# Copying the attention context out of PSUM in two VectorE operations, with the zero column set by GpSimd

## The chip, the cores and the metric

The kernel runs on one core of a Trainium2 chip. The metric is the device time of one execution in microseconds (us). The engines that matter here are TensorE (PE; its weight loads are shown apart as PEld), VectorE (DVE), ScalarE (ACT), GpSimd (POOL) and the DMA queue of SyncE (SP). Each engine works through its own queue of instructions in order and waits at an instruction until the semaphores it names have been raised by the others.

## The reference

A block of cross attention with a feed-forward part, for 128 sequences of 128 tokens with 256 channels, 16 heads of 16 channels, all in float32. The mask is strict (`mask` is 0 below): a token attends only to earlier tokens, so the first token of a sequence attends to none, and its attention row is set to zero.

```python
q = (query @ Wq + bq).reshape(b, s, N_HEADS, D_K).transpose(0, 2, 1, 3)
...
scores = jnp.einsum('bhqd,bhkd->bhqk', q, k) / jnp.sqrt(jnp.float32(D_K))
allowed = j < i + mask
scores = jnp.where(allowed, scores, NEG_INF)
attn = jax.nn.softmax(scores, axis=-1)
attn = attn.at[:, :, 0, :].set(0.0)
ctx = jnp.einsum('bhqk,bhkd->bhqd', attn, v)
...
attn_out = ctx @ Wo + bo
x = layer_norm(query + attn_out, ln1_g, ln1_b)
ffn = jax.nn.relu(x @ W1 + b1) @ W2 + b2
out = layer_norm(x + ffn, ln2_g, ln2_b)
```

The context of the first token is therefore zero in every sequence and every head.

## The kernel before

The 128 sequences are taken in 64 pairs p. The steps of several pairs are interleaved: step p works on the scores of pair p, the context and output projection of pair p - 2, the first feed-forward product of pair p - 3 and p - 4, the second of p - 4 and p - 5, and the projections of pair p + 1. Steps 9 to 60 come from a loop, `for p in range(9, 61): step(p)`; what comes before and after is written out by hand.

The order of the work is fixed by hand. The schedule is manual, and `step` goes through a list of keys, `ORDER`, and calls for each key a small function that issues its instructions. Each engine's queue holds its instructions in just the order in which they are issued, whatever they wait for. The stretch of the list around the change reads (a suffix -1 means the pair of one step earlier):

```python
weigh addbo re0-2 vr-1 hf-2 re2-2 re1-2 turnx-1 xc2-1 re3-2 context scores res0 ro3-2
ro0-2 br1 maskA0 ro2-2 add3 oc0 ro1-2 v1 maskA1 oc2 maskB hs0-1 o1 max3 vk1 vk0 q1
lowmax eh7 oc1 v2 br0 xs2-1 qk w1-1 hs1-1 ok eh6 tokc-1 w2-1 tokx vk2 el3 oc3 hs3-1 v3
add1 el4 w5-1 max1 br3 el0 add2 o2 cc0 wk-1 eh3 k1 finish1-1 ...
```

What these keys do, as far as the prediction speaks of them:

- `weigh` multiplies the exponentials with the values on TensorE (L586, L596) into a PSUM bank. The columns of that bank are ordered by half of the channels, sequence, and token, where the token's index is split as l, q, a (2 x 2 x 32).
- `context` (function at L607) multiplies that bank with `inv`, the inverse sums of the softmax, into the tile `cxT` in SBUF, on VectorE. `cxT` is one tile (128 partitions x 512 columns) for the whole kernel; it is set to zero once at the start (L146 to L148). The column of the first token (l = q = a = 0) of each of the four column groups is never written after that, and so stays zero. For that the function writes the half with q = 1 in one operation of 256 columns (L612) and the half with q = 0 in two (L617): 4 x 31 columns without the first token, and 4 x 32.
- `res0` and `res1` (L1608) make on GpSimd the residual of the second half, `x1b`, from the normed tokens `x1` of pair p - 3, in two operations of 512 columns.
- The matrix products use Strassen's scheme in its form with seven products, so sums and differences of blocks of the operands are formed on GpSimd: `oc0` to `oc3` of `cxT` (L1534), `cc0` to `cc3` of the turned context tokens `cT` (L1534), `xc` of `xT`, `hs` of the hidden layer (`hS`, L1547), `xs` of `x1` (`xS`, L1636). TensorE reads them in `o1` to `o4` (output projection; `o1` takes `cxT` and `oc0`), `k1` to `k4` (keys; `k1` takes `cc0`), `q1` to `q4`, `w1` to `w7` and `h1` to `h7`, most of them at L1147 and L1358.
- `scores` are the products of queries and keys (L440); `maskA0`, `maskA1` and `maskB` add the mask on VectorE (L464, L456).

Of the kernel before, what the change touches and what calls it, by code (L numbers as in the profile page):

```python
# [10 lines left out]
ALU = mybir.AluOpType  # L11
# [8 lines left out]
def tile_cross_attention_block(  # L20
# [22 lines left out]
    nc = tc.nc  # L43
# [101 lines left out]
    cxT = const.tile([P, KC, 2, P], F32, tag="cxT", name="cxT")  # L145
# [460 lines left out]
    def context(p):  # L606
        if "inv" in states[p]:  # L607
            parts = "p (m s l q a) -> p m s l q a"
            pc = states[p].pop("pc").rearrange(parts, m=KC, s=2, l=2, q=2)
            to = cxT.rearrange("p m s (l q a) -> p m s l q a", l=2, q=2)  # L610
            inv = states[p].pop("inv")
            nc.vector.tensor_tensor(  # L612
                to[:, :, :, :, 1], pc[:, :, :, :, 1], inv[:, :, :, :, 1], ALU.mult
            )
            for l in range(2):
                at = slice(1 - l, 32)
                nc.vector.tensor_tensor(  # L617
                    to[:, :, :, l, 0, at], pc[:, :, :, l, 0, at], inv[:, :, :, l, 0, at], ALU.mult
                )
            return  # L620
        pc = states[p].pop("pc").rearrange("p (u i) -> p u i", i=P)
        nc.scalar.copy(cxT.rearrange("p m s i -> p (m s) i")[:, :, 1:], pc[:, :, 1:])
# [1015 lines left out]
    def bring_part(p, n):  # L1638
# [4 lines left out]
        "weigh": lambda p: weigh(p - 2),  # L1643
        "scores": lambda p: scores_both(p),
        "context": lambda p: context(p - 2),
        "deviations": lambda p: scales_of(p),
        "means": lambda p: means_of(p),
# [249 lines left out]
    exponential(1, 1, ONE)  # L1897
    weigh(0)
    context(0)
    project_queries(2)  # L1900
    maximum(1, 1, TWO)
# [62 lines left out]
    weigh(1)  # L1964
    bring(2, nc.sync, EVERY[:8])
    context(1)
    residual1(0)
    scores(3, 1)
# [1124 lines left out]
```

## Time and profile before

| | |
|---|---|
| time, median of 3 runs | 1478.79 us (1475.64 to 1478.85) |
| span of the profiled execution, first to last instruction | 1476.0 us |
| TensorE matmul / weight load busy | 1450.0 us (98%) / 1394.3 us (94%) |
| VectorE busy | 1372.8 us (93%) |
| ScalarE busy | 1304.3 us (88%) |
| GpSimd busy | 1266.4 us (86%) |
| context on VectorE, 256 columns (L612) | 59 operations, median 424 ns |
| context on VectorE, 124 and 128 columns (L617) | 118 operations, median 277 ns |

The page gives the profiled execution by its span; it has no other time of its own. It lies 2.8 us below the median of the runs and inside their range.

Rows of the timeline read: start in us from the span's start, duration in us, engine, line, operation, tile written <- tiles read, type of the operands, number of operations that were merged into the row, and in brackets the idle time of the engine just before the row with what ended it. Rows of a view of groups have the count and the minimum, median and maximum in ns. Rows by stretch have: the stretch, its length, and the busy time (with the number of instructions) of PE, PEld, DVE, ACT and POOL, then TensorE's granted clock, the busy share of the DMA engines and GB/s. A row of waits reads: who waited <- for whom, total us, times, longest.

### The profile page before, as it was taken

The page shows a single profiled execution, that of the slowest core. Times are in us where ns is not written, and L with a number is a line of the kernel's source. Part 1 is how long each engine was busy: PE and PEld are TensorE (multiplying, and loading weights), DVE is VectorE, ACT ScalarE, POOL GpSimd, SP SyncE. Part 2 cuts the span into 40 slices and gives each one's busy share as a digit, 9 for nine tenths or more (in the row PEclk, how much of TensorE's full clock was granted, in tenths as well). Part 3 has the DMA queues.
Part 4 walks back from the last instruction along what each step waited for, and adds up shares of the span by engine and source line. Part 5 has one row for each costly group of instructions (what it writes and reads, how often), then busy time and mean ns, then how long its engine had stood idle before and what let it go on. Part 6 is the DMA issues. An engine that isn't in the chain of part 4 may idle for free.

```text
span 1476.0 us, 61938 instructions
## 1 busy us (share of the span) xinstructions
PE 1450.0 (98%) x20713; PEld 1394.3 (94%) x20713; DVE 1372.8 (93%) x3231; ACT 1304.3 (88%) x5559; POOL 1266.4 (86%) x1816
## 2 busy tenths in 40 slices
PE   8999899999999999999999999999999999999998
PEld 7778799999999999999999999999999999999988
DVE  6987999999999999999999999999999999999767
ACT  4659899999999999999999999999999999999743
POOL 5986898988988988988988988888898888887966
PEclk9999999999999999999999999999999999999999
DMA  8274766766766767776766766766776766774541
GB/s 202 66 142 104 178 162 149 159 152 156 167 158 155 154 152 157 169 159 152 165 147 151 166 157 157 163 149 153 163 160 157 161 147 154 163 163 113 130 109 51
DMA packets 367448, 220.33 MB, mean 149 GB/s; under 512 B 279600, under 2 KB 335152, under 8 KB 367152
## 3 DMA queue, kind: packets, MB, share of 16 engines
q1 hardware_dynamic: 364864, 214.27, 63.9%
q8 instruction: 187, 3.06, 0.9%
q10 hardware_dynamic: 2288, 2.11, 0.7%
q14 instruction: 109, 0.89, 0.2%
HBM read 55.06 MB, written 18.09 MB: 50 GB/s over the span
## 4 chain that ended last, share of the span: by engine, by line
PE 72%; ACT 7%; DVE 4%; DMA 3%; SPq 1%; POOL 1%; issue 1%; DVEq 0%; ACTq 0%; POOLq 0%
PE banks L1147 40%; PE banks L1358 20%; PE banks L440 5%; ACT sm L931 5%; PE banks L596 3%; DMA kT<-kr 2%; PE banks L586 2%; PE banks L971 1%; DMA brought<-turned 1%; ACT kr L1213 1%; PE banks L869 0%; PE banks L1044 0%; ACT qT L1175 0%; SPq L552 0%; PE banks L629 0%
## 5 line engine op out<-in xcount | busy, mean ns | idle before, releaser
L931 ACT ACTIVATE sm<-banks,nmx 128x128 f32<-128x128 f32 x944 | 336.8, 383 | 15.8 <-DVE nmx L1558 12.6
L931 ACT ACTIVATE sm<-sm,nmx 128x64 f32<-128x64 f32 x944 | 321.6, 369 | 1.4 <-DVE nmx L920 1.4
L533 DVE STREAM_TRANSPOSE turned<-sm 128x1024 f32<-128x1024 f32 x186 | 217.0, 1213 | 3.3 <-DMA brought<-turned 2.4
L931 ACT ACTIVATION_READ_ACCUMULATOR sm<-banks,nmx 128x1 f32 x944 | 211.4, 224 | 0.0
L931 ACT ACTIVATION_READ_ACCUMULATOR sm<-sm,nmx 128x1 f32 x944 | 207.8, 220 | 0.0
L1147 PE MATMUL banks<-wt,hS 128*128 128x128 f32 x1344 | 177.6, 275 | 0.0
L1358 PE MATMUL banks<-xS,w1t 128*128 128x128 f32 x1344 | 177.2, 275 | 0.0
L1147 PEld LDWEIGHTS banks<-wt,hS 128*128 128x128 f32 x1344 | 163.6, 192 | 0.1
L1358 PEld LDWEIGHTS banks<-xS,w1t 128*128 128x128 f32 x1344 | 163.4, 192 | 0.0
L1558 DVE TENSOR_REDUCE nmx<-banks 128x4 f32<-128x512 f32 x224 | 152.1, 679 | 1.9
L1547 POOL TENSOR_TENSOR hS<-hT 128x512 f32<-128x512 f32 x116 | 147.5, 1273 | 5.4 <-ACT hT L876 2.4
L1358 PE MATMUL banks<-brought,w 128*128 128x128 f32 x896 | 118.2, 275 | 0.0
L1608 POOL TENSOR_TENSOR x1b<-x,g_r 128x512 f32<-128x512 f32 x56 | 72.3, 1291 | 51.0 <-ACT x L703 51.0
L1147 PE MATMUL banks<-w,hT 128*128 128x128 f32 x896 | 109.8, 275 | 0.0
L1358 PEld LDWEIGHTS banks<-brought,w 128*128 128x128 f32 x896 | 109.0, 192 | 0.0
L440 PE MATMUL banks<-kT,qT 32*64 32x128 f32 (+1 forms) x3840 | 100.7, 331 | 6.3 <-DMA kT<-kr 3.7
L1147 PEld LDWEIGHTS banks<-w,hT 128*128 128x128 f32 x896 | 104.8, 192 | 0.1
L440 PEld LDWEIGHTS banks<-kT,qT 32*64 32x64 f32 x3840 | 82.7, 131 | 16.9 <-ACT hT L1399 4.9
L1534 POOL TENSOR_TENSOR oc<-cxT 128x128 f32<-128x128 f32 x112 | 49.0, 457 | 57.9 <-DVE cxT L617 56.9
L1387 ACT ACTIVATE hT<-hT,b1e_c 128x256 f32<-128x256 f32 x224 | 95.7, 509 | 1.2 <-DVE hT L1383 1.1
L1552 DVE TENSOR_TENSOR banks<-banks,neg 128x256 f32<-128x256 f32 x224 | 93.1, 416 | 0.0
L703 ACT ACTIVATE x<-t,nb,sd 128x256 f32<-128x256 f32 x126 | 68.4, 592 | 19.1 <-POOL nb L726 11.9
(322 smaller groups left out, 4841.1 us busy)
## 6 DMA issues: line engine op xcount, KB each, us to landing
brought<-turned SPq DMA_DIRECT2D x936, 128.0 KB, 2.4
out_dram<-t SPq DMA_DIRECT2D x63, 256.0 KB, 4.7
xb<-in_x_dram SPq DMA_DIRECT2D x124, 128.0 KB, 3.2
cb<-in_ctx_dram SPq DMA_DIRECT2D x124, 128.0 KB, 3.2
x<-in_x_dram SPq DMA_DIRECT2D x31, 512.0 KB, 5.4
kT<-kr SPq DMA_DIRECT2D x112, 128.0 KB, 2.7
brought<-turned SPq DMA_DIRECT2D x40, 96.0 KB, 2.2
w<-in_L_xattn_W_dram SPq DMA_DIRECT2D x2, 1024.0 KB, 7.8
```

The source lines that it names most:

```text
L440: nc.tensor.matmul(st["sps", hi][r][s * HP : (s + 1) * HP, m * 2 * n : (m + 1) * 2 * n].rearrange("p (e j) -> p e j", e=2), st["qT"][strip ...
L533: nc.vector.transpose(turned[:, :, at : at + 256].rearrange("p j (n a) -> p n j a", a=32), states[p]["sm", hi].rearrange("p h j -> p (h j) ...
L703: nc.scalar.activation(x1[:, s], t1[:, s], AF.Identity, bias=st["nb", 1][:, s], scale=sd[:, s])
L931: nc.scalar.activation(sm[:, h, :], src, AF.Exp, bias=nmx[:, h : h + 1], scale=1.0, **({"accum_out": st["su"][:, at : at + 1]} if summed e ...
L1147: nc.tensor.matmul(out, left(k) if self.depth > 1 else left, right(k) if self.depth > 1 else right, start=(n == 1 and k == 0), stop=(k == ...
L1358: nc.tensor.matmul(ps[:, i * P : (i + 1) * P].rearrange("p (n a) -> p n a", a=32), left(i), right, start=(n in (1, 2, 5) and i == 0), stop ...
L1387: nc.scalar.activation(self.hT[:, f, at], self.hT[:, f, at] if src is None else src, AF.Relu, bias=b1e_c[:, f : f + 1], scale=1.0,)
L1534: nc.gpsimd.tensor_tensor(c[:, n], left, right, how)
L1547: engine.tensor_tensor(c[:, n], left, right, how)
L1552: nc.vector.tensor_tensor(ps[:, :, HP:], ps[:, :, HP:], neg[:, 1, None, :].to_broadcast([P, 4, HP]), ALU.add)
L1558: nc.vector.tensor_reduce(states[p]["nmx", 1][:, 4 * b : 4 * b + 4], banks[:, b].rearrange("p (n j) -> p n j", j=P), AX.X, ALU.max, negate ...
L1608: nc.gpsimd.tensor_tensor(st["x1b"], st["x1b"] if n else st["x1"], (be1b_r if n else g1_r)[:, None, :].to_broadcast([P, 2, D]), ALU.add if ...
```

## The change

The two operations on the half with q = 0 become one over all of its 256 columns, so VectorE now writes the first token's columns as well. GpSimd then sets these four columns (one per column group) to zero again, each time, in an instruction that is issued directly behind VectorE's two, within the same function.

```diff
             pc = states[p].pop("pc").rearrange(parts, m=KC, s=2, l=2, q=2)
             to = cxT.rearrange("p m s (l q a) -> p m s l q a", l=2, q=2)
             inv = states[p].pop("inv")
-            nc.vector.tensor_tensor(
-                to[:, :, :, :, 1], pc[:, :, :, :, 1], inv[:, :, :, :, 1], ALU.mult
-            )
-            for l in range(2):
-                at = slice(1 - l, 32)
+            for q in range(2):
                 nc.vector.tensor_tensor(
-                    to[:, :, :, l, 0, at], pc[:, :, :, l, 0, at], inv[:, :, :, l, 0, at], ALU.mult
+                    to[:, :, :, :, q], pc[:, :, :, :, q], inv[:, :, :, :, q], ALU.mult
                 )
+            nc.gpsimd.memset(cxT[:, :, :, 0:1], 0.0)
             return
```

On GpSimd, around the context of one step of the loop, the queue held before (the names are the tiles written <- read, their numbers count buffers; in brackets the semaphores waited for):

```order
L295 TENSOR_TENSOR x_12322<-x_12322,bov_r 128x512 [waits DMAHW0_49]
L1534 TENSOR_TENSOR xc_12756<-xT_12609 128x128
L1608 TENSOR_TENSOR x1b_12979<-x_28_12876,g_r 128x512 [waits DVE_49,Activation_49]
L1534 TENSOR_TENSOR oc_12990<-cxT 128x128 [waits DVE_49]
L1534 TENSOR_TENSOR oc_12990<-cxT 128x128
L1547 TENSOR_TENSOR hS_13002<-hT 128x512 [waits PE_49,Activation_49]
L1534 TENSOR_TENSOR oc_12990<-oc_12990,cxT 128x128 [waits Pool_49]
```

and it now holds (lines behind the change are 3 lower):

```order
L295 TENSOR_TENSOR x_12322<-x_12322,bov_r 128x512 [waits DMAHW0_49]
L1531 TENSOR_TENSOR xc_12756<-xT_12609 128x128
L616 MEMSET cxT 128x4 [waits DVE_49]
L1605 TENSOR_TENSOR x1b_12979<-x_28_12876,g_r 128x512 [waits Activation_49]
L1531 TENSOR_TENSOR oc_12990<-cxT 128x128 [waits DVE_49,Pool_49]
L1531 TENSOR_TENSOR oc_12990<-cxT 128x128
L1544 TENSOR_TENSOR hS_13002<-hT 128x512 [waits PE_49,Activation_49]
L1531 TENSOR_TENSOR oc_12990<-oc_12990,cxT 128x128 [waits Pool_49]
```

The memset stands ahead of `x1b`, because `context` comes before `res0` in the list of keys; the wait for VectorE, which stood at the first `oc`, now stands one operation of 512 columns earlier.

On TensorE, where the output projection begins, the queue held before:

```order
L1147 MATMUL banks<-wv,cT_9419 128x128
L1147 MATMUL banks<-wvt,cc_9463 128x128
L253 NO_OP x3
L1147 MATMUL banks<-wo,cxT 128x128 [waits DVE_49]
L1147 MATMUL banks<-wo,cxT 128x128
L1147 MATMUL banks<-wot,oc_9813 128x128 [waits Pool_49]
```

and it now holds:

```order
L1144 MATMUL banks<-wv,cT_9419 128x128
L1144 MATMUL banks<-wvt,cc_9463 128x128
L253 NO_OP x3
L1144 MATMUL banks<-wo,cxT 128x128 [waits DVE_49,Pool_49]
L1144 MATMUL banks<-wo,cxT 128x128
L1144 MATMUL banks<-wot,oc_9813 128x128 [waits Pool_49]
```

Nothing moved there; the first product on `cxT` has a second semaphore to wait for, that of GpSimd.

## The prediction

> **What bounds the kernel now.** I read the page's engine shares first, then the chain of waits, then the same shares in two stretches (540 us of the loop, and one step).
>
> ```profile
> PE 1450.0 (98%) x20713; PEld 1394.3 (94%) x20713; DVE 1372.8 (93%) x3231; ACT 1304.3 (88%) x5559; POOL 1266.4 (86%) x1816
> PE 72%; ACT 7%; DVE 4%; DMA 3%; SPq 1%; POOL 1%; issue 1%; DVEq 0%; ACTq 0%; POOLq 0%
> ...
> 800.00:1340.00 540.00, 538.00 (x8088) 527.05 (x8087) 520.75 (x1267) 509.49 (x2232) 475.21 (x706) 1.00 0.69 156
> 804.94:826.96 22.02, 22.02 (x337) 21.58 (x334) 21.29 (x53) 20.88 (x93) 19.57 (x29) 1.00 0.73 169
> ```
>
> PE is busy for all 22.02 us of a step at a granted clock of 1.00; GpSimd (POOL) has the most room, 22.02 - 19.57 = 2.45 us. That room makes the change look free, so I looked at where it lies. The view of who waited for whom, for POOL:
>
> ```profile
> POOL oc L1534 <- DVE cxT L617: 56.9, 54, 1.5
> POOL x1b L1608 <- ACT x L703: 51.0, 51, 1.4
> ```
>
> About 1.05 us per step goes before `oc`, which waits for the context, and 1.0 us before `x1b`, the first residual product, which stands ahead of `oc`. The rest of POOL's step has no room. The timeline of POOL, VectorE (DVE) and TensorE (PEld is its weight load) around one context:
>
> ```profile
> 803.11 0.46 POOL L1534 TENSOR_TENSOR xc<-xT 128x128 f32<-128x128 f32 x1
> 804.94 1.29 POOL L1608 TENSOR_TENSOR x1b<-x,g_r 128x512 f32<-128x512 f32 x1 [1.37 <-ACT x L703]
> 806.41 0.42 DVE L612 TENSOR_TENSOR cxT<-banks,brought 128x256 f32<-128x256 f32 x1
> 806.75 0.47 DVE L617 TENSOR_TENSOR cxT<-banks,brought 128x124 f32<-128x124 f32 x2
> 807.14 0.42 DVE L464 TENSOR_TENSOR sm<-banks,neg 128x256 f32<-128x256 f32 x1
> 807.30 0.87 POOL L1534 TENSOR_TENSOR oc<-cxT 128x128 f32<-128x128 f32 x2 [1.07 <-DVE cxT L617]
> 808.19 1.27 POOL L1547 TENSOR_TENSOR hS<-hT 128x512 f32<-128x512 f32 x1
> 808.53 0.53 PEld L1147 LDWEIGHTS banks<-wo,cxT 128*128 128x128 f32 x4
> 808.98 0.30 PEld L1147 LDWEIGHTS banks<-wot,oc 128*128 128x128 f32 x2
> 809.42 0.46 POOL L1534 TENSOR_TENSOR oc<-oc,cxT 128x128 f32<-128x128 f32 x1
> 809.83 0.46 POOL L1636 TENSOR_TENSOR xS<-brought 128x128 f32<-128x128 f32 x1
> 810.25 1.28 POOL L1547 TENSOR_TENSOR hS<-hS,hT 128x512 f32<-128x512 f32 x1
> 811.48 0.47 POOL L1534 TENSOR_TENSOR oc<-cxT,oc 128x128 f32<-128x128 f32 x1
> 811.89 1.28 POOL L1547 TENSOR_TENSOR hS<-hT,hS 128x512 f32<-128x512 f32 x1
> 813.12 0.47 POOL L1534 TENSOR_TENSOR cc<-cT 128x128 f32<-128x128 f32 x1
> 814.11 0.30 PEld L1147 LDWEIGHTS banks<-cc,wkt 128*128 128x128 f32 x2
> ```
>
> From `oc` at 807.30 to `cc` at 813.12 POOL runs without a gap. TensorE takes the first `oc` 808.98 - (807.30 + 0.46) = 1.22 us after it is done (0.46 is the length of the like operations), and the first `cc` 814.11 - 813.59 = 0.52 us after. That 0.52 us is the narrowest place on which this forecast rests.
>
> **The change, term by term.** In VectorE's queue the two operations of 124 and 128 columns become one of 256. Starts are 0.34 us apart behind the 256-column operation (806.41 to 806.75) and the whole context holds VectorE for 0.73 us (to 807.14); two operations of 256 hold it for 2 x 0.34 = 0.68 us. The context ends at 806.75 + 0.42 = 807.17 instead of 806.75 + 0.47 = 807.22: 0.05 us sooner. VectorE works beside a full TensorE, so this gain alone is worth no more than 0.05 us a step. [...]
>
> In POOL's queue the order of instructions shows the memset ahead of `x1b`, and it must wait for VectorE's second operation. So everything that is queued behind it now waits for the context too: first `x1b` (1.29 us), which used to run while POOL had nothing else to do, and behind that `oc`, `hS`, `xS` and `cc`. The memset itself is not in this loop; the nearest rows are POOL's at the start of the program:
>
> ```profile
> 0.72 0.10 POOL L144 MEMSET power<- 128x4 f32 x1 [0.29 <-POOLq L3074]
> 0.75 0.20 POOL masks.py:197 MEMSET ident<- 128x128 f32 x1
> ```
>
> The same four columns, contiguous, take 0.10 us and the next starts after 0.03; 128 columns take 0.20. The bounds are 0.03 and 0.20 us, and I take 0.10, the duration of the row with the same count. Below nothing is excluded, since it is work added to one queue.
>
> `oc` started 807.30 - 807.22 = 0.08 us after the context. The memset then starts at 807.17 + 0.08 = 807.25, `x1b` at 807.35, and `oc` one operation of 512 columns later, 1.24 us by the starts of the two that follow each other here:
>
> ```profile
> 800.63 1.28 POOL L1608 TENSOR_TENSOR x1b<-x1b,be1b_r 128x512 f32<-128x512 f32 x1
> 801.87 1.28 POOL L295 TENSOR_TENSOR x<-x,bov_r 128x512 f32<-128x512 f32 x1
> ```
>
> That is 808.59, or 1.29 us late (bounds 1.22 and 1.39 with the memset's). POOL has no gap before `cc`, so `cc` ends at 813.59 + 1.29 = 814.88. How long after that TensorE starts is bounded by two places where it stood waiting for POOL:
>
> ```profile
> 1451.28 0.46 POOL L1636 TENSOR_TENSOR xS<-xS,cb 128x128 f32<-128x128 f32 x1
> 1451.79 0.30 PEld L1044 LDWEIGHTS banks<-xS,w1t 128*128 128x128 f32 x2 [0.71 <-POOL xS L1636]
> ...
> 43.89 1.90 POOL L500 TENSOR_TENSOR turned<-turned,rs 128x1024 f32<-128x1024 f32 x1
> 46.01 0.31 PEld L569 LDWEIGHTS banks<-ident,turned 128*128 128x128 f32 x3 [0.64 <-POOL turned L500]
> ```
>
> 0.05 us behind the operation of this size, 0.22 us behind a larger one; I take 0.10, nearer the first. TensorE would load `cc` at 814.98 instead of 814.11 and stand still for 0.87 us, a part of it (808.59 + 0.46 + 0.10 - 808.98 = 0.17 us) already at `oc`. The matmuls on `cxT` itself have to wait for the memset, done by 807.35, well before 808.53. The pause is the delay plus the start behind POOL less the 0.52 us that were spare; with the bounds of both it lies between 1.22 + 0.05 - 0.52 = 0.75 and 1.39 + 0.22 - 0.52 = 1.09 us.
>
> Is the pause paid back within the step? A pause that is already there answers it:
>
> ```profile
> 783.85 0.42 DVE L612 TENSOR_TENSOR cxT<-banks,brought 128x256 f32<-128x256 f32 x1
> 784.31 1.05 PE L440 MATMUL banks<-kT,qT 32*64 32x128 f32 x33 [0.53 <-DMA kT<-kr]
> ```
>
> From 783.85 to the next context at 806.41 are 22.56 us, 0.53 more than 22.03: it was not paid back. The next value that is late after `cc` is its last part, due 1.07 us after it is made:
>
> ```profile
> 816.83 0.46 POOL L1534 TENSOR_TENSOR cc<-cT,cc 128x128 f32<-128x128 f32 x1
> 818.36 0.30 PEld L1147 LDWEIGHTS banks<-cc,wk 128*128 128x128 f32 x2
> ```
>
> After the first pause TensorE comes 0.87 us later and POOL 1.29, which leaves 1.07 + 0.87 - 1.29 = 0.65 us: no second pause.
>
> The loop runs p from 9 to 60, 52 steps with this order: 52 x 0.87 = 45.2 us. Pauses that lie between a context and `cc` run beside POOL's work and are swallowed by the new one:
>
> ```profile
> PE banks L440 <- DMA kT<-kr: 3.7, 6, 0.9
> PE banks L440 <- ACT hT L1399: 0.5, 2, 0.3
> ```
>
> So 45.2 - 4.2 = 41 us remain. Outside the loop I add nothing. The last memset waits for the context that ends near 1430.3 and holds back two operations on `t`; behind them POOL stood idle anyway:
>
> ```profile
> 1426.13 1.27 POOL L758 TENSOR_TENSOR t<-t,g_r 128x512 f32<-128x512 f32 x1 [1.86 <-ACT t L740]
> ...
> 1435.24 0.23 POOL L651 TENSOR_SCALAR ve<-mv 128x2 f32<-128x2 f32 x1 [6.49 <-DVE mv L645]
> ```
>
> The profiled execution's span is 1476.0 us and would become 1517. The runs shown have their median 2.8 us above that span, so the forecast is 1478.8 + 41 = 1520 us, slower by 2.8%. With the pause's bounds it is 1478.8 + 52 x 0.75 - 4.2 = 1514 to 1478.8 + 52 x 1.09 - 4.2 = 1531.
>
> **The rivals.**
>
> *It is not slower.* If VectorE, busy for 21.29 of 22.02 us, sets the step, the 0.05 us saved there counts, 52 x 0.05 = 2.6 us, and the time is 1476. It decides if POOL's delay stays below 0.52 us, which would need `x1b` to take some 0.4 us instead of 1.29. For it speaks POOL's 2.45 us of room in each step; against it, that the room lies before the memset, not between it and `cc`.
>
> *Only `oc` is felt.* If POOL made up its delay between `oc` and `cc`, the pause would be the 0.17 us at `oc`, 52 x 0.17 = 9 us, 1488. Against it: the unbroken rows from 807.30 to 813.12.
>
> *The memset is dear.* If it held POOL 0.5 us, the pause grows by 0.4 and the time to 1520 + 52 x 0.4 = 1541. Neither of the two rows above is near that, though neither writes four columns that lie 128 apart.
>
> *The pauses cost TensorE its clock.* In the stretch with its long wait near the end the granted clock was down; where it paused for shorter times it was not:
>
> ```profile
> 150.00:158.00 8.00, 5.96 (x42) 5.10 (x42) 6.52 (x18) 8.00 (x46) 6.07 (x10) 1.00 0.82 185
> 1425.00:1428.00 3.00, 1.12 (x44) 1.13 (x48) 0.00 (x0) 1.52 (x4) 1.79 (x2) 0.68 0.65 161
> ```
>
> At 0.68 over 3 us a pause would cost 0.96 us more, 52 x 0.96 = 50 us, 1570. The first row, 2.04 us of idle in 8 at 1.00, speaks against it. [...]
>
> That the memset stands elsewhere than the source has it is excluded by the order of instructions.
>
> **Chances.** Forecast 0.76; not slower 0.08 (0.03 of it faster, 0.05 the same); `oc` alone 0.06; dear memset 0.07; clock 0.03. A difference counts from 0.3%, 4.4 us, about what a measurement of this kernel can tell. So faster 0.03, same 0.05, slower 0.92. The likeliest case's own 1514 to 1531 is widened toward its neighbours, to 1505 and 1538, for the unknown start after POOL and the unseen memset.
>
> **What would show it.** Right: in the changed loop POOL's `x1b` starts behind the memset with POOL idle for about 3 us before the memset; `oc` starts 1.3 us later against the context; TensorE waits for POOL's `cc` in nearly every step, some 0.9 us, and contexts lie 22.9 us apart. VectorE's busy time falls by about 59 x 0.05 = 3 us. Wrong: a step still near 22.0 us, or a wait that TensorE shows elsewhere than at `cc`.

## The result, and the profile after

| | before | after |
|---|---|---|
| time, median | 1478.4 us (1475.6 to 1478.9) | 1501.0 us (1500.7 to 1501.8) |
| span of the profiled execution | 1476.0 us | 1498.8 us |
| the 52 steps of the loop, from the trace | 1150.1 us | 1172.6 us |
| usual step, up to 860 us | 22.03 us | 22.37 to 22.39 us |

The changed kernel is slower: after to before 1.016, with a 95% interval of 1.0146 to 1.0175, or 22.6 us. The forecast was 1520 us with a range from 1505 to 1538. The sign and the place were right; the time lies 4 us below the range. A step is counted here from the end of the context on VectorE to the end of the next. Of the 22.8 us between the two spans 22.5 lie in the 52 steps of the loop.

The engine shares and the chain of waits of the changed kernel's page, which answer to the first two lines of the prediction:

```profile
PE 1458.8 (97%) x20713; PEld 1396.0 (93%) x20713; DVE 1372.7 (92%) x3172; ACT 1310.1 (87%) x5559; POOL 1266.4 (84%) x1875
PE 55%; POOL 14%; DVE 6%; ACT 5%; DMA 4%; issue 3%; SPq 1%; POOLq 0%; DVEq 0%; ACTq 0%
```

POOL had 1% of the chain and has 14%, though its busy time is the same to the tenth: it is on the path because of when it works, not how much. "issue", time in which an engine waits for nothing that the profile shows, went from 1% to 3%. That is the first trace of something that the prediction didn't have. The longest of POOL's waits:

```profile
POOL cxT L616 <- DVE cxT L613: 140.8, 57, 5.6
```

Both waits of POOL, for `x1` and for the context, have become one at the memset, 2.5 us on average and 2.8 us in the step shown below. The waits of TensorE's weight loads between 270 and 860 us, and between 970 and 1340 us:

```profile
PEld banks L1144 <- POOL cc L1531: 6.1, 19, 0.4
PEld banks L440 <- ACT hT L1396: 4.6, 6, 1.0
PEld banks L1144 <- DVE sm L464: 4.5, 26, 0.2
```

```profile
PEld banks L440 <- ACT hT L1396: 4.6, 5, 1.2
PEld banks L1144 <- DVE sm L464: 4.2, 15, 1.2
PEld banks L1144 <- issue: 3.6, 7, 0.7
PEld banks L440 <- issue: 1.8, 2, 0.9
```

In the first stretch TensorE waits for POOL's `cc`, as forecast, but for about 0.33 us a time and not 0.87. In the second stretch no wait for `cc` is listed; TensorE stands at other places, up to 1.2 us, for "issue" or for a `sm` that had long been done. The rows for `hT` are the same pauses before the scores that the matmuls' view puts down to the keys (`kT`); the kernel before has them too (1.6 us in 2 times and 1.7 in 3 in the same stretches), and what makes them come and go stays open below. Most steps are 22.37 to 22.39 us in the first stretch; in the second they reach 23.1 us.

The timeline of one step of the first stretch, for VectorE, POOL and the weight loads around `cc`:

```profile
814.85 0.76 DVE L613 TENSOR_TENSOR cxT<-banks,brought 128x256 f32<-128x256 f32 x2
815.59 0.42 DVE L464 TENSOR_TENSOR sm<-banks,neg 128x256 f32<-128x256 f32 x1
...
815.33 0.10 POOL L616 MEMSET cxT<- 128x4 f32 x1 [2.82 <-DVE cxT L613]
815.40 1.28 POOL L1605 TENSOR_TENSOR x1b<-x,g_r 128x512 f32<-128x512 f32 x1
816.63 0.87 POOL L1531 TENSOR_TENSOR oc<-cxT 128x128 f32<-128x128 f32 x2
817.46 1.27 POOL L1544 TENSOR_TENSOR hS<-hT 128x512 f32<-128x512 f32 x1
...
822.39 0.47 POOL L1531 TENSOR_TENSOR cc<-cT 128x128 f32<-128x128 f32 x1
...
822.05 0.53 PEld L1144 LDWEIGHTS banks<-cT,wk 128*128 128x128 f32 x4
822.91 0.30 PEld L1144 LDWEIGHTS banks<-cc,wkt 128*128 128x128 f32 x2 [0.34 <-POOL cc L1531]
```

The context's two operations run from 814.85 to 815.61; one of them takes 0.42 us, so the first is done at 815.27. The memset starts at 815.33, 0.06 us behind the first and before the second is done. It doesn't wait for the second. POOL takes `x1b` behind it, as the queue has them: `x1b` starts 0.07 us behind the memset's start, where before it ran 1.47 us ahead of the context (804.94 against 806.41).

### The profile page after: what moved, and what is told of

Its sections match the earlier page's. It is cut to its first block, busy times and chain, and to the rows that moved or that the text cites. A ratio compares the mean times of both kernels' runs of the same rounds, so it can differ in the third digit from the quotient of the medians.

```text
span 1498.8 us, 61994 instructions
## 1 busy us (share of the span) xinstructions
PE 1458.8 (97%) x20713; PEld 1396.0 (93%) x20713; DVE 1372.7 (92%) x3172; ACT 1310.1 (87%) x5559; POOL 1266.4 (84%) x1875
## 4 chain that ended last, share of the span: by engine, by line
PE 55%; POOL 14%; DVE 6%; ACT 5%; DMA 4%; issue 3%; SPq 1%; POOLq 0%; DVEq 0%; ACTq 0%
PE banks L1144 30%; PE banks L1355 17%; POOL hS L1544 6%; DMA kT<-kr 4%; ACT sm L928 3%; PE banks L440 3%; POOL oc L1531 1%; POOL xS L1633 1%; POOL cc L1531 1%; PE banks L968 1%; PE banks L596 1%; DVE turned L1611 1%; DVE hT L1380 1%; DVE hT L1394 1%; DVE cxT L613 1%
## 5 line engine op out<-in xcount | busy, mean ns | idle before, releaser
L616 POOL MEMSET cxT<- 128x4 f32 x59 | 6.2, 105 | 140.8 <-DVE cxT L613 140.8
L1290 DVE TENSOR_TENSOR t<-banks,x1b 128x256 f32<-128x256 f32 x168 | 53.1, 316 | 48.8 <-PE banks L1144 38.6
```

Source lines behind the costliest of these rows:

```text
L1290: nc.vector.tensor_tensor(to, src, of, ALU.add)
```

## The experiments

`EMPTY` is the table with the number of NO_OPs that TensorE's queue gets behind each named product. Where an expectation says that a NO_OP stands in front of `v1` or `h4`, it is the one issued behind that product; behind `v1` stand 3 in the kernels before and after the change. All runs, each with the kernel before on the same chip (medians 1475.5 us for rows 1, 2, 3 and 5, 1476.0 for rows 4 and 6 to 8, 1474.8 for the last three; the table has what the run is, its median, its ratio to before with the 95% interval, and the sum of the 52 steps of the one execution that was profiled):

| run | us | ratio | 52 steps, us |
|---|---|---|---|
| after, one NO_OP less per step | 1490.9 | 1.0099 (1.0077 to 1.0122) | 1163.7 |
| the same, memset behind `x1b` | 1476.4 | 1.0003 (0.9989 to 1.0018) | 1145.4 |
| after, one NO_OP less, other half first | 1512.9 | 1.0253 (1.0233 to 1.0273) | 1184.1 |
| after, without the memset | 1474.7 | 0.9996 (0.998 to 1.0012) | 1147.8 |
| before, one NO_OP more per step | 1486.3 | 1.0063 (1.0041 to 1.0085) | 1159.5 |
| before, one NO_OP moved | 1474.1 | 0.9996 (0.998 to 1.0011) | 1147.7 |
| before, one NO_OP less per step | 1485.8 | 1.0083 (1.0058 to 1.0107) | 1157.3 |
| before, two NO_OPs more per step | 1505.3 | 1.0208 (1.0189 to 1.0228) | 1175.9 |
| before, 52 NO_OPs once ahead of the loop | 1527.4 | 1.0363 (1.034 to 1.0386) | 1197.0 |
| before, 256 once | 1495.9 | 1.0151 (1.0124 to 1.0177) | 1148.2 |
| before, 204 once | 1505.4 | 1.022 (1.0195 to 1.0244) | 1159.2 |

### What the late pauses come from: one instruction per step

The order of TensorE's instructions showed that the first product on `cxT` has two semaphores to wait for in the changed kernel. In its trace an instruction that only waits (EVENT_SEMAPHORE) stands ahead of that product: in the step above it starts at 816.71 us and the product's first weight load at 816.91; the kernel before has none there. The traces count 12 such instructions in a step of TensorE, instead of 11 before, beside 101 NO_OPs and 164 products. The trace of the kernel before has 328 weight loads and 328 matmuls in a step, two of each a product, 656 for the 164; with the rest that was 768 instructions in a step, 3 x 256, and is 769. The DMA view of the changed kernel for 270 to 1340 us has this row (packets, MB, share):

```profile
q8 instruction: 142, 2.33, 1.0%
```

That is 2.33 MB / 142 = 16.4 KB a packet, and 142 packets in 1070 us are 3 in each step of 22.6 us, so a packet holds a third of a step, some 256 instructions. That they are TensorE's, the totals show: the trace of the kernel before has 47926 TensorE instructions and 187 of these packets, 256.3 to each, and with 256 NO_OPs more it has 48182 and 188.

The theory: with 768 the borders between these loads lie at the same places in every step, and with 769 one instruction earlier in each step than in the one before, until one lies where TensorE runs out of instructions. One NO_OP less, in the changed kernel:

```diff
     EMPTY = {
...
-        'v1': 3,
+        'v1': 2,
...
     }
```

> The changed kernel, with one NO_OP less in each of the 52 loop steps on TensorE (3 instead of 4 stood behind the first products of the values: v1 has 2 instead of 3). Theory: the second semaphore that the product on cxT now waits for costs TensorE one instruction more per step, so a step no longer takes three instruction loads of 256 exactly; the loads move along the step by one instruction each time and, from about 970 us on, hold TensorE up behind the scores (the steps of 22.6 to 23.4 us there, 7.3 us more in all than at 22.39). With the count mended, steps stay at 22.39 us to the end and the time falls to about 1494 us. Rival: the long steps late in the loop come from the DMA traffic that the delayed GpSimd sets off (the kT transfers); then one NO_OP does nothing and the time stays at 1501 us.

Measured 1490.9 us, 9 us less than the changed kernel by the ratios (1.016 and 1.0099), and 8.9 us less in the loop's 52 steps. The waits of the weight loads for `cc`, and of the matmuls for the keys:

```profile
PEld banks L1144 <- POOL cc L1531: 16.8, 49, 0.9
```

```profile
PE banks L440 <- DMA kT<-kr: 1.1, 3, 0.6
```

All steps but one (22.60) are 22.36 to 22.39 us now, to the end of the loop, and 48 of the 52 wait for `cc` (one of the 49, the longest, lies behind the loop). The late waits are gone with one NO_OP less, an instruction that does no work. The other way round, one NO_OP more in the kernel before (`'v1': 4`):

> The kernel before, with one NO_OP more in each of the 52 loop steps on TensorE, and nothing else. Theory of the instruction loads: the same late steps become long without any memset, about 12 us in all, 1490 us, and steps before 900 us stay at 22.03. Rival (the memset's delay is all there is): 1478 us, no step changes.

Measured 1486.3 us, 10.8 us more (9.4 in the loop). Here no memset and no second wait exists, so the count alone costs it. The rows for 970 to 1340 us, where the kernel before has at most 0.3 us at a time in rows of this kind:

```profile
PEld banks L1147 <- issue: 4.3, 16, 0.8
PEld banks L440 <- issue: 2.2, 3, 1.1
```

The two parts add up: 1.0099 x 1.0063 = 1.0163, against 1.016 for the changed kernel. The trace of the changed kernel does not put the whole second part at the borders, though. Its loop lies 8.8 us above 52 steps of 22.38 us: 4.3 us in the 13 steps with a late pause of this kind (no wait for `cc` is seen in them), and 4.5 in 16 steps with a wait for `kT`. The kernel before has 4.5 us above its usual steps, nearly all of it in steps with such a wait; with one NO_OP less the waits for `kT` sum to only 1.1 us. So in these single executions some 4 us are seen at the borders, and the rest of the 8.9 goes with the waits for `kT`.

Is it the count or the NO_OP's own place? The next kernel has the NO_OP more behind `v1`, and one less behind `h4` (`'h4': 4`), so 768 again:

> The kernel before with one TensorE NO_OP more in front of 'v1' (3 becomes 4) and one less in front of 'h4' (5 becomes 4): the instructions of a step of the loop stay 768, three loads of 256. Theory (the number of TensorE instructions in a step matters, since the loads drift when it is not a multiple of 256): as the kernel before, about 1475 to 1478 us, every step 22.03 us to the end of the loop, no waits at the weight loads late in the loop. Rival (the NO_OP costs time at its own place, before 'v1'): as the kernel before with one NO_OP more there, about 1486 us, the last twenty steps 22.2 to 23.2 us.

Measured 1474.1 us, ratio 0.9996, and no pause above 0.6 us in the loop, the longest before the scores: it is the count, not the NO_OP's own place. With one NO_OP less than before (`'v1': 2`), 767, the borders drift the other way:

> The kernel before with one TensorE NO_OP less in front of 'v1' (3 becomes 2): 767 instructions in a step, so that the loads of 256 instructions come one instruction later in each step, 52 later by the end of the loop, instead of earlier. Theory (a load costs a pause only where the place it drifts to leaves TensorE short of instructions, and the places that hurt lie on the other side): about 1475 to 1478 us, steps of 22.03 us to the end. Rival (any count that is not a multiple of 256 costs): about 1486 us, with steps above 22.2 us late in the loop.

Measured 1485.8 us: the rival holds, drift toward later places costs as well. But it costs at another place, the product of the weights and the values at the end of the step, and mostly in every second step. The row of the waits, and the weight loads of one such step:

```profile
PEld banks L596 <- issue: 7.1, 12, 1.0
```

```profile
1275.42 0.33 PEld L596 LDWEIGHTS banks<-brought,vz 128*32 128x32 f32 x17
1276.73 0.27 PEld L596 LDWEIGHTS banks<-brought,vz 128*32 128x32 f32 x15 [0.98 <-issue]
```

TensorE stops in the middle of a run of like instructions, after 17 of 32, where nothing is to be waited for. With 770 instructions a step (`'v1': 5`) the drift is twice as fast:

> The kernel before with two TensorE NO_OPs more in front of 'v1' (3 becomes 5): 770 instructions in a step, so that the loads drift by two instructions in each step, 104 by the end of the loop. Theory (the pause comes when the drift has reached some 30 instructions): the long steps, which began about 30 steps into the loop with 769, begin about 15 steps in (near 570 us instead of after 860), and there are about twice as many; with the 10.8 us that one NO_OP cost, about 1497 to 1505 us if the places beyond a drift of 52 cost as much, 1481 to 1486 if they cost nothing. Rival (each NO_OP costs its own time of some hundredths of a microsecond, spread over all steps): two cost twice what one does, 1497 us too, but then every step is longer by 0.4 us from the first one on.

Measured 1505.3 us. The long steps begin near 630 us and stay above 22.5 from 698 us on; with 769 they began between 860 and 970. So the start moves the right way, though later than the 570 us expected, and the early steps are 22.03 us, which excludes the rival. The pause doesn't go away again further on. The row of the waits, and one step of the middle, where TensorE stops five weight loads before the end of the scores:

```profile
PEld banks L440 <- issue: 25.5, 31, 1.5
```

```profile
833.95 1.30 PEld L440 LDWEIGHTS banks<-kT,qT 32*64 32x64 f32 x59
836.42 0.20 PEld L440 LDWEIGHTS banks<-kT,qT 32*64 32x64 f32 x5 [1.16 <-issue]
```

Where the packets lie in a step is read from the trace (start of each packet against the end of the context, median of steps 3 to 10 of the loop and of its last ten; "after, 768" is the changed kernel with one NO_OP less):

```
us                      steps 3 to 10            last ten steps
before, 768          -0.99   4.23  15.65      -0.88   4.48  15.87
after, 769           -0.82   4.73  15.19      -1.13   4.30  13.76
after, 768           -0.83   4.62  16.01      -0.92   4.71  16.04
before, 769          -0.80   4.25  14.95      -1.20   4.23  13.28
before, 767          -0.91   4.85  15.32      -0.06   6.27  17.62
before, 770          -0.88   4.19  14.23      -1.64   2.69  12.65
```

With 768 they stay, with 769 and 770 they go to earlier places, with 767 to later ones. And each pause stands in a fixed relation to a packet: in the kernel with 770, 29 pauses of over 0.3 us at the scores or at `wv,cT` end 1.23 to 1.55 us after the end of the packet before them. One such step of the changed kernel, by its timeline and by the DMA view of 1266 to 1268 us; the one packet in that view lies at 1266.23 to 1267.57, and TensorE goes on 1.42 us later:

```profile
1266.46 1.37 PEld L440 LDWEIGHTS banks<-kT,qT 32*64 32x64 f32 x64
1268.99 0.52 PEld L1144 LDWEIGHTS banks<-wv,cT 128*128 128x128 f32 x4 [1.17 <-DVE sm L464]
```

```profile
q8 instruction: 1, 0.02, 4.2%
```

The trace names `sm` as the releaser, but in every step without a pause this load starts 0.64 us after the context ends. `sm` is the nearest event, not the cause.

If the place of the borders is all that counts, then it can be moved once for all, without a change of the steps. Three kernels put NO_OPs ahead of the loop, the first of them 52:

```diff
+    empty(52)
     for p in range(9, 61):
         step(p)
```

> The kernel before with 52 more TensorE NO_OPs once, right ahead of the loop; the steps themselves keep their 768 instructions. Theory (what counts is where in a step the borders between loads of 256 instructions lie): the borders lie from the first step on where one instruction more per step brought them only at the end of the loop, 52 earlier. With 770 instructions a step that place was reached at the 26th step, and the steps there were 23.18 and 23.01 us long; all 52 steps would be about 22.9 us (22.6 to 23.2), 52 x 0.87 = 45 us more (30 to 60), about 1521 us (1506 to 1536). Rival (the steps grow only when their count of instructions is not a multiple of 256): steps of 22.03 us, and the 52 NO_OPs cost at most 52 x 0.03 = 1.5 us once (a step has 768 instructions in 22.03 us), 1476 to 1478 us.

Measured 1527.4 us. The theory's numbers hold: all 52 steps are 22.76 to 23.60 us, from the first on, though each has its 768 instructions. TensorE's row of waits, to be held against 2.0 us in 7 times before, and one of the pauses, two weight loads before the scores' end:

```profile
PEld banks L440 <- issue: 43.0, 58, 1.4
```

```profile
304.17 1.42 PEld L440 LDWEIGHTS banks<-kT,qT 32*64 32x64 f32 x62
306.14 0.19 PEld L440 LDWEIGHTS banks<-kT,qT 32*64 32x64 f32 x2 [0.56 <-issue]
```

With 256, a whole load, the borders should be back where they were:

> The kernel before with 256 more TensorE NO_OPs once, right ahead of the loop: a whole load more, so that the borders lie in the steps where they lay before. Theory: steps of 22.03 us; what is added is the NO_OPs' own time, once, between 256 / 110 = 2.3 us (TensorE takes some 110 instructions per us in its fastest stretch, the scores) and 256 x 0.029 = 7.4 us (its mean in a step): 1478 to 1484 us. Rival (NO_OPs ahead of the loop hurt by themselves, not by the place of the borders): more than the kernel with 52, by some 256 / 52 times.

The steps are 22.03 us again and sum to 1148.2 us, as the theory has it. The time, 1495.9 us, is not what was expected, since the price of a NO_OP was wrong: the first step behind them is 44.21 us long, 19.75 us longer than before, and TensorE's loads there stand still:

```profile
204.33 0.44 PEld L586 LDWEIGHTS banks<-brought,vd 128*32 128x32 f32 x16 [18.86 <-issue]
```

That is 19.75 / 256 = 0.077 us a NO_OP where many stand together; the 52 lengthened the same step by 3.6 us, 0.069 each. TensorE's granted clock was lower meanwhile: 0.66 between 184.0 and 204.3 us and 0.54 in the 3.7 us behind, where the kernel before has 1.00, and back at 1.00 from 208 us on. What such a NO_OP costs at the full clock is not shown. Both bounds of the expectation, 0.009 and 0.029 us, came from rows of real instructions, and neither held. Within a step they are covered: the usual early step with 767, 769 and 770 instructions is 22.03 us. With 204, 52 short of a load:

> The kernel before with 204 more TensorE NO_OPs once, right ahead of the loop: 256 less 52, so that the borders lie 52 instructions later in every step, where 767 instructions a step brought them at the end of the loop. Theory: the steps are like the late ones there, a pause of 0.4 to 1.0 us at the product of weights and values in about every second step, 22.03 and 22.3 to 23.1 us in turn; 52 x 0.25 = 13 us (8 to 25) and the NO_OPs' own 1.9 to 6 us more, 1485 to 1505 us. Rival (it grows with the number of NO_OPs): between the kernels with 52 and with 256, steps 22.03 us.

Measured 1505.4 us. The NO_OPs cost 16.0 us; the steps are 22.03 us with longer ones, up to 23.3, between them, and TensorE stops at `vz` (9.1 us in 13 times), as with 767. The sum over the loop is 9.1 us above before, at the lower end of what was expected. So the same number of instructions costs nothing, 9 or 47 us in the loop, depending only on where the borders lie.

One count ties these runs together. Number the instructions of TensorE's queue in each trace from the first one on, and take the remainder by 256. In the six kernels whose borders were moved (changed, 769, 767, 770, 52 and 204), 121 pauses of over 0.3 us in the loop stand behind a remainder of 193 or 194, at five different products, and each ends 1.20 to 1.63 us after the end of a packet. In the seven others (the kernel before, 256 once, and all the rest with 768) no pause stands there. Of the other pauses above 0.3 us, all but two stand before the scores or at `cc`, where a semaphore is waited for. So these pauses stand at one fixed place in the count of 256, whichever of the five products stood there.

Why those places hurt was not tried by itself. What the rows show: TensorE takes instructions unevenly. The products of `vd`, `vz` and the scores, 160 weight loads and 160 matmuls, are 320 of the 768 instructions and go through in about 2.9 us (804.79 to 807.70 us in the kernel before), 110 a us, the other 448 in 19. The packets ahead of the 121 pauses took 0.9 to 1.6 us, and TensorE went on 2.2 to 2.9 us after the start of the packet. That is as long as those 320 instructions last. So the likely reason, argued and not shown: a border that moves a packet's start into the dense stretch, and the need for it to just behind, leaves no time. In the kernel before, a packet that starts at -0.99 us would, by the same 2.2 to 2.9 us, be of use from 1.2 to 1.9 us after the context, and no pause shows that it was needed sooner. What a border costs is measured: nothing that shows where the borders lie as in the kernel before, and up to 1.4 us a time where they were moved.

### What the memset waits for

In the changed kernel the half with q = 0, which holds the zero column, is written first. The next kernel writes it second, on top of the kernel with one NO_OP less:

```diff
-            for q in range(2):
+            for q in (1, 0):
```

> As e1, with VectorE's two operations in the other order, so that the half with the zero column is written last and the memset has to wait for the second operation, as the prediction had assumed. Theory: the pause grows by the 0.34 us by which the second operation starts later, steps become 22.73 us, 52 x 0.34 = 18 us more than e1, about 1512 us. If the memset waits for both operations whatever their order, the time is that of e1, 1494 us.

Measured 1512.9 us, 22 us more than with the halves in their order; the steps are 22.76 us. The timeline of one:

```profile
801.28 0.76 DVE L613 TENSOR_TENSOR cxT<-banks,brought 128x256 f32<-128x256 f32 x2
...
802.16 0.10 POOL L616 MEMSET cxT<- 128x4 f32 x1 [2.82 <-DVE cxT L613]
802.22 1.28 POOL L1605 TENSOR_TENSOR x1b<-x,g_r 128x512 f32<-128x512 f32 x1
803.46 0.87 POOL L1531 TENSOR_TENSOR oc<-cxT 128x128 f32<-128x128 f32 x2
...
803.97 0.30 PEld L1144 LDWEIGHTS banks<-wot,oc 128*128 128x128 f32 x2
809.72 0.30 PEld L1144 LDWEIGHTS banks<-cc,wkt 128*128 128x128 f32 x2 [0.54 <-POOL cc L1531]
```

The memset starts 0.88 us after the first operation here, 0.12 us behind the end of the second, and 0.48 after it in the changed kernel. The 0.40 us (0.34 were expected) come out as 22.76 - 22.37 = 0.39 us in each step. This is the wait that the prediction had assumed.

### The memset's place in POOL's queue, and VectorE's part alone

The memset goes behind the first operation on `x1b`, everything else as in the kernel with one NO_OP less:

```diff
+    def zero(p):
+        nc.gpsimd.memset(cxT[:, :, :, 0:1], 0.0)
+
-    def context(p):
+    def context(p, whole=True):
...
-            nc.gpsimd.memset(cxT[:, :, :, 0:1], 0.0)
+            if whole:
+                zero(p)
...
+        "copied": lambda p: context(p - 2, False),
+        "zero": lambda p: zero(p - 2),
...
-        weigh addbo re0-2 vr-1 hf-2 re2-2 re1-2 turnx-1 xc2-1 re3-2 context scores res0 ro3-2
+        weigh addbo re0-2 vr-1 hf-2 re2-2 re1-2 turnx-1 xc2-1 re3-2 copied scores res0 zero ro3-2
```

> As e1, and in the loop the memset is issued behind x1b (res0) instead of ahead of it. Theory (x1b, kept back by the memset's wait, makes oc, hS and cc late): the delay is gone, oc starts 0.08 us behind the context again, steps are 22.0 us and the time is that of before less 52 x 0.05 us, about 1476 us. Rival (the price is the memset itself or TensorE's second wait): about 1494 us as in e1.

Measured 1476.4 us, no difference from before. POOL, in one step:

```profile
800.32 1.29 POOL L1609 TENSOR_TENSOR x1b<-x,g_r 128x512 f32<-128x512 f32 x1 [0.88 <-ACT x L704]
802.28 0.10 POOL L607 MEMSET cxT<- 128x4 f32 x1 [0.66 <-DVE cxT L616]
802.69 0.87 POOL L1535 TENSOR_TENSOR oc<-cxT 128x128 f32<-128x128 f32 x2 [0.31 <-DVE cxT L616]
```

`x1b` runs again while POOL waits for the context, and POOL is idle on both sides of the memset, which costs nothing there. So the 15 us of the first experiment are the place of the memset, not its work. Last, the changed kernel without the memset (the first token's columns are not set to zero):

```diff
-            nc.gpsimd.memset(cxT[:, :, :, 0:1], 0.0)
```

> The changed kernel without GpSimd's memset: the column of the first token is not set to zero (this part of the computation is left out); the two operations of 256 columns on VectorE stay. The product on the context then waits for VectorE alone, so that a step has 768 TensorE instructions again, and POOL's queue is as before the change. Theory (the whole loss came from the memset's place and from the second wait; VectorE's part alone is worth the 0.06 us by which its two operations end sooner): steps of 21.97 us, 52 x 0.06 = 3 us less than before, about 1473 to 1476 us, ratio 0.998. Rival (VectorE's 0.06 us never reaches the end): 1475 to 1478 us, ratio 1.000, steps 22.03.

Measured 1474.7 us, ratio 0.9996: between the two expectations, and apart from neither. In the traces of both kernels the usual step is 21.97 us, 0.06 less than before, so the gain that the prediction allowed VectorE is there; 52 x 0.06 = 3 us are 0.2%, which these runs can't tell from nothing. No kernel here is measurably faster than the kernel before.

## Where the prediction was right, and where it failed

The path of one step, each point counted from the start of the context's first operation (forecast: from the prediction's rows, with 806.41 as the zero; measured: 814.85 in the timeline above):

| us after the context's first operation starts | forecast | measured |
|---|---|---|
| memset starts | 0.84 | 0.48 |
| `x1b` starts | 0.94 | 0.55 |
| `oc` starts | 2.18 | 1.78 |
| `cc` ends | 8.47 | 8.01 |
| TensorE loads `cc` | 8.57 | 8.06 |

- **The step that failed: "it must wait for VectorE's second operation".** The memset waits for the first alone, whose half it writes into; 0.36 us of the forecast 0.87 are gone with that. The order shown in the document names only the engine waited for, not which of its operations, and the prediction took the one issued last. The experiment with the halves exchanged shows that wait and its price, +0.39 us a step.
- **Terms of the sum that were too large.** The next operation starts 0.07 us behind the memset's start, not 0.10 (0.03 us; with `x1b`'s length another 0.01). From `oc` to the end of `cc` it took 6.23 us, not 6.29. TensorE starts 0.05 us behind `cc`, not 0.10, the lower of the two bounds shown. Together 0.15 us (and the rival "not slower" sets its bound at a delay of 0.52 us without that start behind POOL; with the prediction's own 0.10 it is 0.42). 0.87 - 0.36 - 0.15 = 0.36 us, and the steps up to 860 us are 0.34 to 0.36 us longer.
- **The sum over the loop** is that of the kernel with one NO_OP less: 52 x 0.345 = 17.9 us (steps of 22.37 to 22.38), less the pauses that are swallowed. The prediction had 4.2 us for these; the loop before lay 1150.1 - 52 x 22.03 = 4.5 us above its usual steps. That leaves 13.4 us; the traces have 13.6 in the loop, and the medians 15.4.
- **What was missing: a term for one more instruction on TensorE.** "Nothing" was added there but a second semaphore, which the prediction took for free since the memset is done in time. It is free as a wait: the kernel with the memset behind `x1b` has it too, with one NO_OP less, and no loss. As an instruction it moves the borders: with one NO_OP less the loop is 8.9 us shorter, some 4 us of it in steps with a pause at a border, the rest in steps with waits for `kT`. The waits "elsewhere than at `cc`", which the prediction named as what would prove it wrong, are these. The two errors pull in opposite directions: without the missing term the changed kernel would take some 1493 us (1.0099 x 1478.4), 12 us below the range and not 4. That the forecast came this near is in part luck.
- **VectorE's busy time** was to fall by 3 us and fell by 0.1. The two operations hold VectorE for 0.74 us until `sm` starts (0.73 before), not for 2 x 0.34 = 0.68: the start behind the second comes later than the start behind the first. The context still ends 0.05 us sooner, and the step is 0.06 us shorter where nothing else is in the way.
- **Right:** the cause of the loss in the place of `x1b` behind the memset, POOL without a gap from `oc` to `cc`, TensorE's wait at `cc`, once in a step as long as the late pauses don't take its place, no second pause in a step, nothing lost outside the loop, and no clock lost (the mean granted clock is 0.997). None of the rivals came about; the time lies between the likeliest case (1514 to 1531) and the rival that only `oc` is felt (1488), where no case was worked out.

Open is what makes the waits for the keys (`kT`) come and go: 3.7 us in 6 times before, 9.3 in 14 after, 1.1 in 3 with one NO_OP less. With the NO_OP moved it is 0.8 in 2 and without the memset 5.0 in 6, though neither has the late pauses, so the late pauses are not all of it.

## What to carry to other kernels

Before pricing a wait that moves, find the one instruction that it waits for: here it was the operation that writes the same half of the tile, not the last one issued by that engine, and the difference was 0.39 us a step. When an instruction is put into another engine's queue, ask what stands behind it that used to run earlier, and put it behind work that is ready: with the memset ahead of `x1b` the kernel with one NO_OP less took 1490.9 us, behind it 1476.4. And count a loop's instructions on TensorE before and after a change, with those that a second semaphore adds: in this loop, with 768 a step in packets of 256, one more or one less moved the borders of the instruction loads through the step and cost 0.6% and 0.8%. Look for "issue" behind dense runs of small matmuls, where it stood here.

## What the runs showed of the hardware that was not expected

- TensorE's instructions came in packets of 16.4 KB, three in a step of 768. At a border in a bad place TensorE stood for up to 1.4 us, 47 us over 52 steps in the worst case tried (52 NO_OPs ahead of the loop), and the pauses ended 1.2 to 1.6 us after the end of a packet.
- NO_OPs on TensorE cost nothing that shows among the products in a step (the usual early step is 22.03 us with 767 to 770 instructions), and 0.07 to 0.08 us each where 52 to 256 of them stood together, at a granted clock that fell to 0.66 in the longest run of them.
- Between the start of GpSimd's memset of four columns and the start of the next operation lay 0.06 to 0.07 us, less than the 0.10 us that the memset lasts; it lasts 0.10 us with its columns 128 apart, as it did with the contiguous four of the program's start.
